# Two-layer transformer kernel: k, v and beta projected ahead of the first scan, q inside it; gates made at once; the last tile's loads and two layer-1 pieces placed later

## The chip, the cores and the metric

The kernel runs on one NeuronCore of a Trainium2 chip. The metric is the time of one execution on the device, in microseconds. Before the change it is 2255.97 us, the median of three runs (2253.57 to 2258.22).

The core has five engines, each with its own instruction queue, worked through in order: TensorE (PE, matrix products and transposes), VectorE (DVE), ScalarE (ACT, activation functions from tables that have to be loaded), GpSimd (POOL) and SyncE (SP). DMAs are issued here from the SP queue and from GpSimd's queue. All data is float32.

## The reference, cut to what matters

Eight sequences of 512 tokens with 256 features go through two layers. Layer 0 is a delta-rule attention, with a state of 16 x 16 per head that is updated token by token, followed by a mixture of eight experts with one expert per token. Layer 1 is a softmax attention with a position bias, followed by eight gated experts. Each branch is added to x with a gate made from a conditioning vector.

```python
mod = (silu(c) @ wmod).reshape(8, 6, 1, 256)          # for each layer
sa, ca, ga, sb, cb, gb = (mod[:, j] for j in range(6))
ga = (2 * (ga >= 0) - 1) * maximum(abs(ga), 0.25)     # gb alike
h = layernorm(x) * (1 + ca) + sa
q = l2norm(silu(h @ Wq.T)); k = l2norm(silu(h @ Wk.T))   # per head of 16
v = silu(h @ Wv.T); beta = sigmoid(h @ Wbeta.T)
def step(M, (q_t, k_t, v_t, b_t)):                    # over 512 tokens
    out_t = q_t @ M
    M = M + b_t * outer(k_t, v_t - M @ k_t)
x = x + ga * (rmsnorm(outs) @ Wo.T)
h = layernorm(x) * (1 + cb) + sb
x = x + gb * expert[argmax(h @ gate_w.T)](h)          # relu(h w1 + b1) w2 + b2
# layer 1: softmax attention, then gated experts, in the same frame
```

## The kernel before, in words

**Tiles and scans.** The tokens are cut into four tiles of 128 (index i), and a tile holds these 128 positions of all eight sequences (index b, called examples). For each tile `front(i, at)` makes q, k, v and beta, `heads` turns K and V so that the 128 pairs of example and head lie on the partitions, and `scan(i, K, V)` runs 128 steps. A step is four VectorE instructions, each of which needs the one before: product (L640), reduction (L644), product (L650), subtraction (L655). Every eighth step also copies eight columns of V into the buffer `terms` (L638), and every sixteenth one writes V back (L646). The outputs are not made step by step: `attend(i, ...)` makes them with matrix products during the next tile's scan, `route` then finds each token's expert and scatters the rows, and `experts` runs 15 slots of 128 rows. For each slot it loads the rows (L1061, SP queue) and the weights of the slot's expert (`fetch`, L1044, an indirect DMA on GpSimd's queue, two buffers for each of the two parts), multiplies (L1083, L1102), adds a bias on GpSimd (L1108) and stores (L1109, GpSimd's queue). The finished rows are gathered (L1117), multiplied by the gate (L1153) and added to x in memory (L1154), all on GpSimd's queue.

**Order.** The order is written by hand: each piece of work has a place, a step number, and `run` sorts the pieces and puts them between the scan's steps. The place binds VectorE's instructions of the piece to come after that step; the other engines' instructions are ordered by the framework's scheduler, by readiness and by the order of the code. So a piece whose other instructions are ready early can start early on them, while VectorE's instruction sits at its step and is waited for, or waits.

**front.** For the first tile (i = 0) everything runs ahead of the scan: `stats_first` (layer norm statistics of all eight examples), then for each example `turn` (normalise on ScalarE, L140; transpose, L143; scale and shift on ScalarE, L145), `project` (L535: 512 columns, q and k; L539: 272 columns, v and beta; silu, copy and squares on ScalarE) and `squares` (sums of squares by head on VectorE, L553). `roots` takes sigmoid and square roots on ScalarE and `scales` multiplies q, k and v by their factors per head (L588), for tile 0 on VectorE and GpSimd in turns, for the others on GpSimd. For tiles 1 to 3 the same pieces run inside the previous tile's scan, from step 30 (tile 1) or 47, with `stats` on ScalarE and `normal` (L517, L518) on VectorE.

**Gates.** `gate_rows` is called four times in the first scan (steps 6, 8, 14, 16): a matrix product gives 8 rows of 256, ScalarE copies them, four VectorE instructions make sign and magnitude (L367 to L370), and a DMA stores them for `load_gates` at step 26.

**The last tile.** `experts(3)` begins with the load of `x_last` (L1036), in a buffer of the tag `yrow`, of which there are two; the gathers of tile 2 use the same two buffers. In its middle it loads three tiles of x for layer 1 (L1113). `prologue` makes layer 1's first k, q and v from them: 14 pieces, of which the first eight (k = 0 to 7) are placed at 102 + 4k among the expert slots (placed at 10j), and the others at 201 + k. The pieces k = 6 and 7 are `both` (L261), q and k of the first three tiles.

Of the kernel before, what the change touches and what calls it, by code (L numbers as in the profile page):

```python
# [19 lines left out]
P = 128  # L20
B = 8
# [42 lines left out]
def tile_two_layers(ctx: ExitStack, tc: tile.TileContext, t: dict, out: bass.AP):  # L64
# [217 lines left out]
    with ExitStack() as l0:  # L282
# [68 lines left out]

        def gate_rows(layer, branch):

            wm = wms[layer, branch]
            pg = bank()
            for k in range(2):
                nc.tensor.matmul(
                    pg[:B, :D], scs[layer][:, k, :], wm[:, k, 2 * D :],
                    start=(k == 0), stop=(k == 1),
                )  # L360
            name = f"{layer}{branch}"
            g, sign, mag, gt = (
                fp.tile([B, D], F32, tag=tag, name=f"{tag}_{name}", bufs=2)
                for tag in ("hslot", "yrow", "ysb", "hTs")
            )
            nc.scalar.copy(g, pg[:B, :D])
            nc.vector.tensor_scalar(sign, g, 0.0, 2.0, ALU.is_ge, ALU.mult)  # L367
            nc.vector.scalar_tensor_tensor(mag, g, -1.0, g, ALU.mult, ALU.max)
            nc.vector.tensor_scalar_max(mag, mag, 0.25)
            nc.vector.scalar_tensor_tensor(gt, sign, -1.0, mag, ALU.add, ALU.mult)  # L370
            nc.gpsimd.dma_start(mod_d[f"g{name}"], gt)
# [77 lines left out]
        def front(i, at):  # L449
# [102 lines left out]
            def squares(b):  # L552
                nc.vector.tensor_reduce(  # L553
                    ss[:, :, b, :], got["sq", b].rearrange("p s (n d) -> p s n d", d=HD),
                    AX.X, ALU.add,
                )


            n = B if i == 0 else B // 2
# [8 lines left out]
            def scales(h):  # L568
                bs = slice(h * n, (h + 1) * n)
                nc.vector.tensor_scalar_add(ss[:, :, bs], ss[:, :, bs], 1e-6)  # L570
                nc.vector.reciprocal(ss[:, :, bs], ss[:, :, bs])
                nc.vector.tensor_mul(ss[:, 1, bs], ss[:, 1, bs], beta[:, bs])
                todo = [
                    (b, of)
                    for of in ((1, 2, 0) if i == 0 else ((1, 2, 0),))
                    for b in range(h * n, (h + 1) * n)
                ]
                for b, of in todo:
                    for which in of if i else (of,):
                        x, by = (  # L580
                            (qk[:, 0, b, :], ss[:, 0, b, :]),
                            (qk[:, 1, b, :], ss[:, 1, b, :]),
                            (v[:, b, :], beta[:, b, :]),
                        )[which]
                        view = x.rearrange("p (n d) -> p n d", d=HD)

                        ve = nc.vector if i == 0 and which and b % 2 else nc.gpsimd
                        ve.tensor_mul(view, view, by.unsqueeze(2).to_broadcast([P, NH, HD]))  # L588
# [18 lines left out]
            pieces = []  # L607
            for p in range(B // 2):
                if i > 0:
                    pieces.append((at + 8 * p, lambda p=p: stats(p)))  # L610
                    pieces.append((at + 8 * p + 4, lambda p=p: normal(p)))
                elif p == 0:
                    pieces.append((at, stats_first))
                for c in range(2):
                    b = 2 * p + c
                    pieces.append((at + 8 * p + 3 * c + 4, lambda b=b: turn(b)))

                    late = 4.5 if i == 0 else 0
                    pieces.append((at + 8 * p + 3 * c + 4 + late, lambda b=b: project(b)))
                    pieces.append((at + 8 * p + 3 * c + 11, lambda b=b: squares(b)))  # L620
            for h in range(B // n):
                last = at + 16 * h + (23 if i else 39)
                pieces.append((last, lambda h=h: roots(h)))
                pieces.append((last + 2, lambda h=h: scales(h)))
            pieces.append((at + 46, lambda: heads("K", qk[:, 1], 1.0)))
            pieces.append((at + 49, lambda: heads("V", v, -1.0)))
            got["qk"] = qk
            return got, pieces
# [28 lines left out]
        def attend(i, qk, V, x1, norms):  # L657
# [198 lines left out]
            for h in range(2):  # L856
                pieces.append((16 * h + 25, lambda h=h: roots(h)))
                for b in range(4 * h, 4 * h + 4):
                    pieces.append((13 * h + 25 + b, lambda b=b: rest(b)))
                    pieces.append((12 * h + 29 + b, lambda b=b: stats(b)))  # L860
# [170 lines left out]
        def experts(i, slot, idx):  # L1031


            if i == NT - 1:
                x_last = fp.tile([P, D], F32, tag="yrow", name="x_last", bufs=2)
                nc.sync.dma_start(x_last, x2d[0][i])  # L1036
# [37 lines left out]
            for j in range(NSLOT):  # L1074
# [36 lines left out]
                if i == NT - 1 and j == NSLOT // 2:  # L1111
                    for k in range(i):
                        nc.sync.dma_start(w1["xs"][:, k, :], x2d[0][k])  # L1113
# [128 lines left out]
        parts, pieces = front(0, 0)  # L1242
        run(pieces)
        rest, gathers = [], []
        for i in range(NT):
# [8 lines left out]
            else:  # L1254
# [9 lines left out]
                    (18, strip_rows),  # L1264
                    (26, load_gates),
                ]
            before = parts
            if i + 1 < NT:
                parts, more = front(i + 1, 47 if i > 0 else 30)
                pieces = pieces + more  # L1270
# [10 lines left out]
        for k, piece in enumerate(begun):  # L1281
            last.append((102 + 4 * k if k < NT + 4 else 201 + k, piece))
# [348 lines left out]
```

## Time and profile before

| | us |
|---|---|
| median of three runs | 2255.97 |
| the profiled execution, its own time | 2256.92 |
| its span, from first to last instruction | 2255.2 |
| before the first scan step (L655 at 66.5) | 66 |
| first to last scan step | about 1040 |
| from there to layer 1's first scores (1401.7) | about 295 |
| layer 1 | about 853 |

The mean granted TensorE clock is 0.864. A line of the timeline has the start in us from the span's start, the busy time in us, engine, line, operation, output and inputs by the program's names with shapes, the number of merged instructions, and in brackets the engine's idle time before it with what released it. "SPq" and "POOLq" are queue instructions. A line of the chain has start and length in us. A line of the waits has who waited for whom, the total in us, the number of times and the longest. A line of the busy times by stretch has the stretch, its length, busy us (and instructions) of PE, PE's weight loads, DVE, ACT and POOL, the granted clock, the DMA engines' busy share and GB/s.

### The profile page before, as it was taken

What the parts mean: (1) busy time and instruction counts of PE and PEld (TensorE: products, weight loads), DVE (VectorE), ACT (ScalarE), POOL (GpSimd) and SP (SyncE); (2) the same over time, 40 slices, a digit from 0 to 9 for tenths busy, and PEclk for the clock granted to TensorE, in tenths of its full rate; (3) what the DMA queues carried; (4) which work ended last, traced back from release to release, by engine and by line L of the source; (5) the groups of instructions that cost most, each with busy time, mean ns of one, the idle gap of its engine ahead of it and who ended that gap; (6) DMA issues with size and microseconds to landing.
All of it is one profiled execution on the core that took longest, in us unless ns stands there. A gap on an engine that the chain in (4) does not pass through costs nothing.

```text
span 2255.2 us, 32318 instructions
## 1 busy us (share of the span) xinstructions
PE 1726.5 (77%) x10874; PEld 1195.3 (53%) x10874; DVE 1595.2 (71%) x4533; ACT 1076.8 (48%) x2672; POOL 589.8 (26%) x791
## 2 busy tenths in 40 slices
PE   5334027479696887939893597999999999999997
PEld 3212025359574785738762596565555555555553
DVE  3899999899987999899652002686675767666654
ACT  5144025465356643613341244877475665747431
POOL 1102014145253453624374443010201011010111
PEclk9566567599798998959996798899999999999998
DMA  5110000178002680138665582000101010100001
GB/s 161 48 45 10 0 1 11 34 263 312 32 13 86 251 309 31 46 143 300 178 112 172 178 315 61 13 12 12 23 14 22 15 29 11 24 12 13 17 17 17
DMA packets 88630, 189.57 MB, mean 84 GB/s; under 512 B 13689, under 2 KB 67105, under 8 KB 75665
## 3 DMA queue, kind: packets, MB, share of 16 engines
q0 software_dynamic: 33696, 137.43, 19.0%
q1 hardware_dynamic: 54768, 50.09, 7.9%
q8 instruction: 86, 1.41, 0.3%
q14 instruction: 80, 0.65, 0.1%
HBM read 175.10 MB, written 36.93 MB: 94 GB/s over the span
## 4 chain that ended last, share of the span: by engine, by line
PE 42%; DVE 26%; issue 14%; ACT 7%; DMA 6%; POOL 5%; SPq 0%; POOLq 0%; ACTq 0%; DVEq 0%
PE ps L1469 6%; DVE state L644 6%; PE ps L1083 5%; PE ps L1330 5%; DVE state L655 5%; DVE terms L640 5%; DVE upd L650 5%; PE ps L1102 4%; PE ps L1304 3%; PE ps L535 3%; PE ps L1351 2%; DMA w<-in_wrows,idx 2%; PE ps L261 2%; DVE sc L1313 1%; PE ps L244 1%
## 5 line engine op out<-in xcount | busy, mean ns | idle before, releaser
L1318 ACT ACTIVATE pr<-sc,low 128x384 f32<-128x384 f32 (+3 forms) x512 | 255.6, 556 | 196.7 <-DVE low L1313 194.5
L1313 DVE CUSTOM_DVE_ANT_0 sc<-ps,strips 128x384 f32<-128x384 f32 (+3 forms) x512 | 225.4, 485 | 87.4 <-PE ps L1304 56.6
L1083 PE MATMUL ps<-hTs,w 128*128 128x128 f32 x1920 | 236.8, 284 | 19.9 <-DMA w<-in_wrows,idx 13.5
L1083 PEld LDWEIGHTS ps<-hTs,w 128*128 128x128 f32 x1920 | 233.3, 200 | 27.2 <-issue 13.1
L644 DVE TENSOR_REDUCE state<-terms 128x16 f32<-128x272 f32 x512 | 227.2, 444 | 15.8
L655 DVE TENSOR_TENSOR state<-state,upd 128x256 f32<-128x256 f32 x511 | 223.1, 437 | 14.8
L1469 PE MATMUL ps<-ew,hTd 128*128 128x512 f32 x512 | 232.9, 608 | 0.0
L640 DVE TENSOR_TENSOR terms<-state,K 128x256 f32<-128x256 f32 x512 | 216.0, 422 | 14.4
L1102 PE MATMUL ps<-w,act 128*128 128x256 f32 x960 | 220.8, 384 | 6.1 <-DVE dm L820 6.1
L650 DVE TENSOR_TENSOR upd<-K,state 128x256 f32<-128x256 f32 x511 | 214.2, 419 | 15.6
L1092 ACT ACTIVATE act<-ps,w 128x128 f32<-128x128 f32 x480 | 137.1, 371 | 152.8 <-PE ps L1083 151.7
L1330 PE MATMUL ps<-cst,pr 128*128 128x128 f32 x1280 | 192.4, 296 | 14.9 <-DVE low L1313 12.5
L1102 PEld LDWEIGHTS ps<-w,act 128*128 128x128 f32 x960 | 180.0, 193 | 29.5 <-DVE dm L820 6.6
L1474 DVE SCALAR_TENSOR_TENSOR accd<-ps,wtd,accd 128x256 f32<-128x256 f32 x256 | 123.8, 483 | 99.8 <-PE ps L1469 87.7
L1330 PEld LDWEIGHTS ps<-cst,pr 128*128 128x128 f32 x1280 | 149.8, 149 | 83.7 <-DVE low L1313 24.2
L1469 PEld LDWEIGHTS ps<-ew,hTd 128*128 128x128 f32 x512 | 96.4, 193 | 121.2 <-issue 107.6
L1478 POOL TENSOR_TENSOR accd<-accd,bc_g 128x256 f32<-128x256 f32 x28 | 20.4, 728 | 528.5 <-DVE accd L1474 528.5
L1044 POOL DMA_INDIRECT w<-in_wrows,idx x120 | 123.2, 1027 | 127.8 <-ACT hTs L1068 55.9
L1304 PE MATMUL ps<-kT,qTc 32*128 32x128 f32 (+3 forms) x1024 | 132.2, 491 | 5.4 <-DVE low L1313 3.8
L1339 DVE COPY prT<-ps 128x512 f32<-128x512 f32 (+3 forms) x256 | 117.0, 484 | 10.4 <-PE ps L1330 10.0
L674 PE MATMUL ps<-cst,V 128*128 128x128 f32 x64 | 12.5, 378 | 124.2 <-DVE V L646 124.2
L1337 ACT COPY prT<-ps 128x512 f32<-128x512 f32 (+3 forms) x256 | 98.9, 414 | 8.6 <-PE ps L1330 8.2
(264 smaller groups left out, 2939.4 us busy)
## 6 DMA issues: line engine op xcount, KB each, us to landing
hs<-zero SPq DMA_DIRECT2D x4, 1920.0 KB
hslot<-hs SPq DMA_DIRECT2D x60, 128.0 KB
ys<-ysb POOLq DMA_DIRECT2D x60, 128.0 KB, 3.8
x<-in_x SPq DMA_DIRECT2D x32, 128.0 KB
strips<-strip_d SPq DMA_DIRECT2D x16, 256.0 KB
out<-accd POOLq DMA_DIRECT2D x32, 128.0 KB, 3.1
wm<-in_wmod SPq DMA_DIRECT2D x4, 768.0 KB
xt<-in_x SPq DMA_DIRECT2D x12, 256.0 KB
```

Source lines behind the costliest of these rows:

```text
L640: nc.vector.tensor_mul(term[:, :, :HD], M, K[:, s, :].unsqueeze(1).to_broadcast([P, HD, HD]))
L644: nc.vector.tensor_reduce(delta, term, AX.X, ALU.add)
L650: nc.vector.tensor_mul(upd, K[:, s, :].unsqueeze(2).to_broadcast([P, HD, HD]), delta.unsqueeze(1).to_broadcast([P, HD, HD]),)
L655: yield nc.vector.tensor_sub(M, M, upd).ins
L1083: nc.tensor.matmul(ph[:, q * P : (q + 1) * P], w[:, k * FF + f * P : k * FF + (f + 1) * P], hT[:, k, :], start=(k == 0), stop=(k == 1),)
L1092: nc.scalar.activation(act[:, f, :], ph[:, q * P : (q + 1) * P], AF.Relu, bias=w[:, 2 * FF + f : 2 * FF + f + 1],)
L1102: nc.tensor.matmul(py[:, :D], act[:, f, :], w[:, f * D : (f + 1) * D], start=(f == 0), stop=(f == NFC - 1),)
L1304: made = nc.tensor.matmul(pscs[r][:, :W], qT[rows, g, o, i * P : (i + 1) * P], kT[rows, g, :W], start=True, stop=True,)
L1313: nc.vector.tensor_tensor_reduce(out=sc[:, :W], in0=pscs[r][:, :W], in1=strips[:, n, S - W :], scale=1.0, scalar=3.0e38, op0=ALU.add, op1= ...
L1318: nc.scalar.activation(pr, sc[:, :W], AF.Exp, bias=low, scale=-1.0)
L1330: nc.tensor.transpose(pt[:, (i - j) * P : (i - j + 1) * P], prs[r, i][:, j * P : (j + 1) * P], ident,)
L1469: nc.tensor.matmul(pe, hT[0][:, k, cols], ew[:, k, e : e + 2, :], start=(k == 0), stop=(k == 1),)
```

## The change

**First tile.** `front` gets pieces of its own for i = 0. `turn_first` normalises on VectorE and scales one half on ScalarE and the other on VectorE. `project_first` projects k, v and beta only; `squares_first` sums k's squares. q is projected, squared, summed and scaled by pieces in the list `later`, placed at steps 1 to 25 of the first scan, with sums and products on GpSimd. `scales_first` gives all v products to GpSimd and all k products to VectorE.

**Sums of squares.** `halved` sums 16 elements by four GpSimd adds on 8, 4, 2 and 1 columns per head. It is used for q of tile 0 and for tile 1; tiles 2 and 3 keep VectorE's reduction.

**Gates.** The four products are copied into one tile at partitions 0, 32, 64 and 96, and `push_gates` (step 20) makes all gates with four VectorE instructions and stores them with four DMAs.

**Places.** For tiles 1 to 3 `normal` comes one step later, `turn` one, `project`, `squares`, `roots`, `scales` and `heads` two; `attend`'s `stats` one. In the last tile `x_last` is loaded at slot 7 with layer 1's x, both behind the row loads issued so far; the pieces k = 6 and 7 of the prologue move to 151 and 152, behind the last slot.

```diff
+        gated = {}
         def gate_rows(layer, branch):
+            if not gated:
+                gated["g"] = fp.tile([P, D], F32, tag="hslot", name="gates", bufs=2)
+                nc.gpsimd.memset(gated["g"], 0.0)
...
-            nc.scalar.copy(g, pg[:B, :D])
+            at = 32 * (2 * layer + branch)
+            nc.scalar.copy(gated["g"][at : at + B, :], pg[:B, :D])
+        def push_gates():
...
             nc.vector.scalar_tensor_tensor(gt, sign, -1.0, mag, ALU.add, ALU.mult)
-            nc.gpsimd.dma_start(mod_d[f"g{name}"], gt)
+            for layer in range(2):
+                for branch in range(2):
+                    at = 32 * (2 * layer + branch)
+                    nc.gpsimd.dma_start(mod_d[f"g{layer}{branch}"], gt[at : at + B, :])
...
+            def turn_first(b):
...
+                nc.vector.tensor_scalar(
+                    xn, xt[:, q, :], rs[:, q : q + 1], off[:, q : q + 1], ALU.mult, ALU.add
+                )
...
+                nc.scalar.activation(
+                    hT[:, 0, :], pt[:, :P], AF.Identity, bias=plus[:, 0], scale=by[:, 0]
+                )
+                nc.vector.tensor_scalar(
+                    hT[:, 1, :], pt[:, P : 2 * P], by[:, 1], plus[:, 1], ALU.mult, ALU.add
+                )
+            def project_first(b):
...
+                for dst, lo, hi in ((pa, D, 2 * D), (pb, 2 * D, NQKV)):
...
+                nc.scalar.activation(qk[:, 1, b, :], pa[:, :D], AF.Silu)
+                nc.scalar.activation(v[:, b, :], pb[:, :D], AF.Silu)
+                nc.vector.tensor_copy(beta[:, b, :], pb[:, D : D + NH])
...
+            def scales_first():
...
+                for b in range(B):
+                    by_head(nc.gpsimd, v[:, b, :], beta[:, b, :])
+                    by_head(nc.vector, qk[:, 1, b, :], ss[:, 1, b, :])
...
+            def halved(dst, sq):
+                for m in (HD // 2, HD // 4, HD // 8):
+                    nc.gpsimd.tensor_add(sq[..., :m], sq[..., :m], sq[..., m : 2 * m])
+                nc.gpsimd.tensor_add(dst, sq[..., 0], sq[..., 1])
...
+            if i == 0:
+                pieces.append((0, stats_first))
+                for b in range(B):
+                    pieces.append((4 * b + 4, lambda b=b: turn_first(b)))
+                    pieces.append((4 * b + 9, lambda b=b: project_first(b)))
+                    pieces.append((4 * b + 13, lambda b=b: squares_first(b)))
+                    later.append((1 + 2 * b, lambda b=b: project_q(b)))
+                    later.append((4 + 2 * b, lambda b=b: squares_q(b)))
+                pieces += [(46, roots_first), (47, scales_first)]
+                later += [(22, roots_q), (25, scales_q)]
...
-                    pieces.append((12 * h + 29 + b, lambda b=b: stats(b)))
+                    pieces.append((12 * h + 30 + b, lambda b=b: stats(b)))
...
-            if i == NT - 1:
-                x_last = fp.tile([P, D], F32, tag="yrow", name="x_last", bufs=2)
-                nc.sync.dma_start(x_last, x2d[0][i])
...
                 if i == NT - 1 and j == NSLOT // 2:
-                    for k in range(i):
-                        nc.sync.dma_start(w1["xs"][:, k, :], x2d[0][k])
+                    x_last = fp.tile([P, D], F32, tag="yrow", name="x_last", bufs=2)
+                    with tc.issue_after(issued["rows"]):
+                        nc.sync.dma_start(x_last, x2d[0][i])
+                        for k in range(i):
+                            nc.sync.dma_start(w1["xs"][:, k, :], x2d[0][k])
...
-            last.append((102 + 4 * k if k < NT + 4 else 201 + k, piece))
+            place = 102 + 4 * k if k < NT + 2 else 145 + k if k < NT + 4 else 201 + k
+            last.append((place, piece))
```

## The prediction

> **What bounds the kernel now.** I read the chain of work that ended last first, then the busy times by stretch, then the timeline of the stretches that the change touches, and the waits there.
>
> ```profile
> PE 42%; DVE 26%; issue 14%; ACT 7%; DMA 6%; POOL 5%; SPq 0%; POOLq 0%; ACTq 0%; DVEq 0%
> 62.70:296.00 233.30, 57.87 (x189) 33.82 (x187) 217.40 (x534) 58.81 (x133) 16.90 (x29) 0.59 0.08 25
> ```
>
> No engine binds all of it. The last line is the first scan: VectorE busy 217.4 of 233.3 us, so a scan is a chain on VectorE, and everything put into its order is paid unless it fits the gaps between dependent instructions. The work before the first scan is bound by TensorE, then by a chain of ScalarE tables and products:
>
> ```profile
> 26.68 1.98 PE L535 MATMUL ps<-wqkv,hT 128*128 128x512 f32 x4 [0.69 <-ACT hT L145]
> 28.50 1.08 PE L539 MATMUL ps<-wqkv,hT 128*128 128x272 f32 x4
> ...
> 33.34 1.98 PE L535 MATMUL ps<-wqkv,hT 128*128 128x512 f32 x4 [0.69 <-ACT hT L145]
> ...
> 53.51 3.12 DVE L588 TENSOR_TENSOR qk<-qk,ss 128x256 f32<-128x256 f32 x4
> ...
> 57.91 3.68 PE L596 MATMUL ps<-cst,qk 128*128 128x128 f32 x16 [12.38 <-POOL qk L588]
> ```
>
> Two examples take 33.34 - 26.68 = 6.66 us; K's transposes wait 12.4 us, at the end for GpSimd, which scales q between its K products (L588, twelve products from 52.63, 8.12 us). The largest hole lies before the experts of the last tile (chain, then timeline, then the SP queue's waits):
>
> ```profile
> 1257.20 3.16 DMA x<-yrow
> 1260.49 0.34 SPq L1036
> 1260.87 3.10 DMA hslot<-hs
> ...
> 1264.10 0.66 PE L1064 MATMUL ps<-cst,hslot 128*128 128x128 f32 x2 [52.81 <-DMA hslot<-hs]
> ...
> SPq L1036 <- DMA x<-yrow: 42.2, 1, 42.2
> ```
>
> TensorE idles 52.8 us for a 128 KB load. That load is queued on SP behind x_last (L1036), and x_last waits 42.2 us, because its buffer (tag yrow, two of them) belongs to the third tile's gathers until their adds have landed. The scattered rows have been in place since about 1217, when the queue issues ew.
>
> **The change, part by part.** The sum is made against the profiled execution: span 2255.2, its own time 2256.9, so 1.7 us around the span. The median of the runs shown is 2256.0, 0.9 less; I take the savings from the profiled execution and give the forecast against the median.
>
> **Opening (turn_first, project_first, scales_first).** Today an example costs TensorE 1.82 us (L535, 26.68 to 28.50) and 0.91 us (L539), a transpose pair 0.30, and half of a 0.69 us wait per pair. Without q's 256 columns it is 0.91 + 0.91 + 0.30 = 2.12 us; turns run two examples ahead, so the wait goes. 3.33 - 2.12 = 1.21 us, seven times, is 8.5 us; the first example runs at the cold price (3.78 us for what costs 1.88 later), and I count nothing for it. ScalarE does four instructions of 0.37 to 0.47 us per example, 1.6 us; VectorE normalises (0.35, as the 128x256 tensor_scalar of L427), turns half (0.4), copies beta (0.17) and reduces half the squares (0.4), 1.3 us; both hide behind 2.12, and would cost the difference if that cover went. Tables and roots (46.3 to 49.6) stay. Then from the root to K's transposes it is 8.3 us. New: add, reciprocal and product at 128 columns, 0.2 + 0.94 + 0.6 = 1.8, and eight K products on VectorE. They cost 0.78 each beside GpSimd (53.51, 3.12 for four) and 0.42 alone; GpSimd's v products last 8 x 0.70 = 5.6 us, so 1.8 + 5.1 = 6.9 us, or 8.0 if something keeps GpSimd busy throughout. Gain 0.3 to 1.4, taken 1.0, since most products have company. **-9.5** (ends -6 and -11).
>
> **First scan.** Two rows of it (timeline of VectorE) and one of a later scan:
>
> ```profile
> 170.14 0.43 DVE L655 TENSOR_TENSOR state<-state,upd 128x256 f32<-128x256 f32 x1
> 170.49 0.67 DVE L553 TENSOR_REDUCE ss<-sq 128x32 f32<-128x512 f32 x1
> ...
> 518.42 3.68 DVE L638 COPY terms<-V 128x128 f32<-128x128 f32 x1
> ```
>
> A bare step is 1.86 us (66.48 to 68.34); this one, with a squares reduction, ends at 172.46 and is 2.32, so it costs 0.46, not 0.67. Eight go to GpSimd: -3.7. A step with four gate instructions is 2.53 (82.53 to 85.06), +0.67; four such groups become one of the same length per partition: -2.0. Added: q's add and reciprocal, +0.7 (the step with add, reciprocal and product is +1.06, of which the product is some 0.35). normal's waits for its root (1.2 us in this scan) are reached a step later: -0.6.
>
> GpSimd gets 40 instructions for q (32 adds, 8 products), 32 adds for tile 1, a memset; TensorE and ScalarE get q's 8 projections, roots. ScalarE is busy 58.8 us of 233 here, so this is hidden, if q's roots are there at step 25. VectorE waits for them there, and the whole scan is queued behind it. Eight projections at the cold price (1.9 us) and eight sums on GpSimd (no row; bounded by 0.61 us, the 128x256 product, for each of four adds, and 0.19, the small memset of L392, so 0.8 to 2.4 us an example, 1.1 taken since sizes halve) are done by about step 12. Tile 1's sums have some 4 us before their scales at step 57.
>
> Here a rule of the Trainium skill matters, and it speaks against the change. The row L638 is a copy of 0.27 us that took 3.68, all through GpSimd's run of products (517.9 to 522.5); at 790.40 another took 4.14. "SBUF — State Buffer", section "Who interferes with whom", has a port pair that VectorE's copies and GpSimd share, as a lock held for the whole instruction. By that a copy loses one GpSimd instruction at most, 0.6 us; by the rows it loses the rest of the run. The rows decide. About 27 us of new GpSimd work over 16 copies in 240 us is two hits: 0.6 us by the rule, up to 5 by the rows if they meet the 4.9 us run of q's products. That run begins at step 26, over by 29, and the copies stand at 24 and 32, so I take +1.2. Sum **-4.4** (ends -7 and 0).
>
> **Later scans: pieces one or two steps later.** The longest waits of the third scan:
>
> ```profile
> DVE stf L840 <- POOL x L832: 4.2, 4, 1.4
> DVE ss L553 <- ACT sq L549: 4.1, 3, 3.5
> ```
>
> The fourth scan has 4.3 on L840 again, the second 2.8 on L553 and 1.8 on L517. stats one step later saves up to 1.86 in each of two scans, the first squares up to 1.9 in two, normal 2.6 in all: -10 at most. What is late next is ScalarE's turn and project behind the later normal, so the squares gain less than their two steps. I take half, **-5**. The two long copies may lie better or worse against a run that starts two steps later: 0, ends -7 and +7.
>
> **Last tile's experts.** x_last moves from the head of experts to slot 7, behind that slot's row loads on SP. The loads follow ew, issued until 1218.2; with ew's 2 MB and three weight fetches in flight I let the first land at 1229, as the third fetch does (1229.7): 35 us earlier than 1264. What is queued behind the moved loads then is the later slots' rows; the gathers have landed by that time, so no wait. But GpSimd's queue is in order, and it is the one with the gathers: per slot a fetch 1.05, add 0.72, store 0.59, fetch 1.0 and four issue gaps of 0.3, so 4.6 of the slot's 7.24 us (1270.51 to 1277.75); the gathers need 8 x (1.0 + 0.74 + 0.95 + 0.9) = 29 us beside it. One end: all gathers go first, only the two slots whose weights are there by 1236.5 run early, and the third's fetch lands at 1268: -14.5 + 3 = -12. Other end: -35. Fetches are issued by readiness (one stands among the gathers at 1230.07), so some slots get through: I take three and a bit, **-22**. DMA has room, but not much: share 0.82 at 300 GB/s from 1265 to 1350.
>
> **q and k of layer 1's first three tiles (L261).** They stand between expert slots where TensorE has no gap:
>
> ```profile
> 1365.00 2.74 PE L261 MATMUL ps<-hTc,wqkv 128*128 128x384 f32 x8
> 1371.15 2.75 PE L261 MATMUL ps<-hTc,wqkv 128*128 128x384 f32 x8
> ```
>
> Moved behind the last slot they lie in the 10.1 us that TensorE waits for the gathered rows (to 1394.7). 2 x 2.58 = **-5.2**; without that cover 0. The gates' four stores at step 20 end at about 103 us; SP waits for them with the gates' load, and the next x tile behind it is not issued before 135.8 today, so 0.
>
> Sum: -9.5 - 4.4 - 5 - 22 - 5.2 = -46; 2256 - 46 = **2210**.
>
> **Rivals.** *GpSimd hands the early start back:* experts and gathers disturb each other, -8 to -12 in place of -22: 2222; for it the in-order queue, against it the fetch at 1230. *The scans' gains are eaten* by copies behind GpSimd runs and ScalarE's order: the 5 of the later scans and the 4.4 of the first gone, one or two long copies (3.5 each) more: 2222 to 2228. *Everything fits:* -34 at the experts, -8 in the scans: 2194. *The change doesn't do what it says* (another load holds SP): 2232. *Slower:* in tiles 1 to 3 the statistics of the next pair now stand between a pair's two projections. ScalarE's pair takes 16.2 us (134.64 to 150.84) against 15.8 of VectorE's steps. If that order forced two further table loads (2 x 1.28) and a second wait for the cold TensorE (2.2), each of 12 pairs would lose 4.8 us: 58, so 2268. It decides from (46 + 4.5) / 12 = 4.2 us a pair. Against: there are two loads a pair now (136.85, 148.61), and the new order also needs only two.
>
> **Chances.** Likeliest 0.55 (own range 2200 to 2220), handed back 0.15, eaten 0.10, everything fits 0.12, not as it says 0.03, slower 0.05. The range 2188 to 2234 holds all but the slow case and some tails. A change under 0.2% (4.5 us) can't be told from none here. Faster 0.94, same 0.01, slower 0.05.
>
> **What would show it.** First scan step at about 56 instead of 65.5; no L553 in the first scan; L1064 of the last tile near 1229 - 19 = 1210 with no SP wait on x<-yrow before it; L261 after the last L1102. It would be wrong if SP still waits there, if GpSimd's fetches come only after the gathers, or if copies of L638 show several microseconds in the first scan.

## The result, and the profile after

The changed kernel takes 2242.51 us (median of 17 runs, 2225.61 to 2246.34); the kernel before, run beside it, 2254.15 us (17 runs, 2248.09 to 2262.81). The ratio is 0.9933, with a 95% interval of 0.9916 to 0.9950: faster by 11 to 19 us. The forecast was 46 us faster, 2210, with a range of 2188 to 2234: the sign is right, the size is not.

The profiled execution took 2237.59 us with a span of 2235.7, so 19.5 less than the span before. The medians differ by 11.6: the profiled execution lies 4.9 us under the median of its runs, that of before 2.8 over its own, and in which part those 8 us lie is not shown. By parts, from the milestones of both traces (the first and last scan step, layer 1's first scores, the end):

| part | before, us | after, us | change | forecast |
|---|---|---|---|---|
| up to the first scan step | 66.5 | 55.6 | -10.9 | -9.5 |
| first scan | 249.7 | 244.9 | -4.8 | -4.4 |
| scans 2 to 4 | 789.7 | 795.4 | +5.7 | -5 |
| last scan's end to layer 1's first scores | 295.9 | 288.4 | -7.5 | -22 and -5.2 |
| layer 1 | 853.5 | 851.5 | -2.0 | 0 |

The first two rows are close to the forecast. This is the first scan in the busy times by stretch:

```profile
55.58:300.44 244.86, 59.37 (x195) 34.54 (x195) 227.15 (x556) 66.48 (x149) 44.80 (x101) 0.61 0.08 23
```

VectorE has 556 instructions here and GpSimd 44.8 us of work; in the whole first scan of before (66.48 to 316.16) it was 573 and 16.9 us. The opening, from the timeline:

```profile
29.64 1.95 PE L595 MATMUL ps<-wqkv,hT 128*128 128x256 f32 x8
31.42 0.38 PE L574 MATMUL ps<-cst,xn_first 128*128 128x128 f32 x2
...
40.73 6.04 POOL L619 TENSOR_TENSOR v<-v,beta 128x256 f32<-128x256 f32 x8 [38.07 <-ACT beta L614]
41.01 6.04 DVE L619 TENSOR_TENSOR qk<-qk,ss 128x256 f32<-128x256 f32 x8
47.20 1.52 PE L694 MATMUL ps<-cst,qk 128*128 128x128 f32 x6 [11.83 <-DVE qk L619]
```

An example costs TensorE 2.0 us (29.64 to 31.64) where 2.12 was forecast, and K's transposes begin at 47.20 in place of 57.91.

The third row went the wrong way. The waits of VectorE in the third scan, which before were led by 4.2 us (`stf`) and 4.1 us (the sums of squares):

```profile
DVE ss L680 <- ACT ss L676: 9.0, 1, 9.0
DVE count L1076 <- PE ps L1071: 3.5, 1, 3.5
DVE dm L925 <- POOL bdM L926: 2.1, 2, 1.4
DVE rsa L529 <- ACT sda L513: 2.0, 2, 1.7
DVE stf L945 <- POOL x L937: 0.9, 1, 0.9
```

The two waits that the change aimed at are down to 0.9 and nothing. At the head stands one that was 0.5 us before (L570 there, L680 now). The second scan has it too, with 10.1 us. Its surroundings, from the timeline:

```profile
450.90 0.69 PE L1166 MATMUL ps<-cst,hslot 128*128 128x128 f32 x2 [11.80 <-DMA hslot<-hs]
...
452.05 6.47 PE L1185 MATMUL ps<-hTs,w 128*128 128x128 f32 x32 [0.46 <-ACT hTs L1170]
...
458.36 0.38 PE L143 MATMUL ps<-cst,xna 128*128 128x128 f32 x2
...
460.11 1.98 PE L547 MATMUL ps<-wqkv,hT 128*128 128x512 f32 x4 [1.36 <-ACT hT L145]
...
465.60 0.31 ACT L676 ACTIVATE ss<-ss 128x128 f32<-128x128 f32 x1
...
465.94 0.23 DVE L680 TENSOR_SCALAR ss<-ss 128x128 f32<-128x128 f32 x1 [10.13 <-ACT ss L676]
```

Read it from the bottom: VectorE waits for a root of ScalarE; ScalarE, in order, has the silu and the squares of the next pair ahead of it; these wait for the pair's transposes and products (L143, L547); and TensorE, in order, first runs an expert slot (L1166, L1185), whose rows came after a wait of 11.8 us. Before, the order on TensorE was the other one:

```profile
463.28 0.69 PE L143 MATMUL ps<-cst,xna 128*128 128x128 f32 x2 [6.82 <-ACT xna L140]
464.52 3.78 PE L535 MATMUL ps<-wqkv,hT 128*128 128x512 f32 x4 [0.55 <-ACT hT L145]
468.09 1.59 PE L539 MATMUL ps<-wqkv,hT 128*128 128x272 f32 x4
469.52 0.38 PE L1064 MATMUL ps<-cst,hslot 128*128 128x128 f32 x2
```

Last, the last tile's experts, TensorE and GpSimd in the timeline:

```profile
1227.18 0.66 PE L1166 MATMUL ps<-cst,hslot 128*128 128x128 f32 x2 [21.83 <-DMA hslot<-hs]
...
1241.39 3.62 PE L1204 MATMUL ps<-w,act 128*128 128x256 f32 x16
...
1253.69 0.92 POOL L1259 DMA_DIRECT2D x<-yrow  x1 [0.30 <-POOL yrow L1258]
1254.91 1.10 POOL L1146 DMA_INDIRECT w<-in_wrows,idx  x1 [0.30 <-issue]
...
1261.00 1.41 PE L1185 MATMUL ps<-hTs,w 128*128 128x128 f32 x5 [15.99 <-DMA w<-in_wrows,idx]
```

The first slot starts 131.3 us after the last scan's end (158.2 before), so 26.9 sooner. Two slots run; then TensorE idles 16.0 us for weights whose fetch GpSimd issues at 1254.91, after its last gather's add. Counted from slot start to slot start, in us:

| slot | 0 | 1 | 2 | 3 to 5 | 6 | 7 to 10 | 11 | 12 | 13 | all 14 |
|---|---|---|---|---|---|---|---|---|---|---|
| before | 8.6 | 7.2 | 7.3 | 7.2 | 7.5 | 7.2 | 10.5 | 10.7 | 9.8 | 112.2 |
| after | 9.3 | 23.4 | 10.0 | 7.2 | 12.7 | 7.2 | 10.4 | 8.1 | 7.3 | 131.9 |

Slots 12 and 13 are shorter by 5.1 us: that is L261, which now lies behind the last slot, in the wait for the gathered rows:

```profile
1367.20 5.32 PE L261 MATMUL ps<-hTc,wqkv 128*128 128x384 f32 x16
1377.57 0.69 PE L179 MATMUL ps<-cst,xnc 128*128 128x128 f32 x2 [5.04 <-ACT xnc L172]
```

So of 26.9 us, 16.2 + 2.7 + 5.2 + 0.7 = 24.8 go back in slots 1, 2, 6 and 0. What delays slot 6 stands in ScalarE's rows (timeline):

```profile
1299.54 0.30 ACT L126 ACTIVATE sdc<-mvc,cst 128x3 f32<-128x3 f32 x1 [6.22 <-DVE mvc L121]
1299.75 1.12 ACT L1194 ACTIVATE act<-ps,w 128x128 f32<-128x128 f32 x4
...
1300.15 5.41 PE L1204 MATMUL ps<-w,act 128*128 128x256 f32 x16 [3.49 <-ACT act L1194]
```

The slot's ReLU (L1194) stands behind a root for layer 1 (L126), which waits for the x tiles that are now loaded only at slot 7. Before, these loads went out at 1261.9, ahead of the first slot.

### The profile page after: what moved, and what is told of

It reads as the page before. It is cut to its first block, busy times and chain, and to the rows that moved or that the text cites. A ratio compares the mean times of both kernels' runs of the same rounds, so it can differ in the third digit from the quotient of the medians.

```text
span 2235.7 us, 32456 instructions
## 1 busy us (share of the span) xinstructions
PE 1727.0 (77%) x10906; PEld 1205.2 (54%) x10906; DVE 1590.3 (71%) x4539; ACT 1090.1 (49%) x2678; POOL 615.1 (28%) x856
## 5 line engine op out<-in xcount | busy, mean ns | idle before, releaser
L1185 PE MATMUL ps<-hTs,w 128*128 128x128 f32 x1920 | 246.6, 291 | 35.2 <-DMA w<-in_wrows,idx 30.0
L1185 PEld LDWEIGHTS ps<-hTs,w 128*128 128x128 f32 x1920 | 242.7, 207 | 42.6 <-issue 32.5
L1194 ACT ACTIVATE act<-ps,w 128x128 f32<-128x128 f32 x480 | 136.8, 372 | 160.9 <-PE ps L1185 147.0
L1146 POOL DMA_INDIRECT w<-in_wrows,idx x120 | 123.6, 1030 | 132.9 <-ACT hTs L1170 64.2
L1446 DVE COPY prT<-ps 128x512 f32<-128x512 f32 (+3 forms) x256 | 117.1, 485 | 10.4 <-PE ps L1437 10.2
```

Of the source, the lines that this page charges most:

```text
L1185: nc.tensor.matmul(ph[:, q * P : (q + 1) * P], w[:, k * FF + f * P : k * FF + (f + 1) * P], hT[:, k, :], start=(k == 0), stop=(k == 1),)
L1194: nc.scalar.activation(act[:, f, :], ph[:, q * P : (q + 1) * P], AF.Relu, bias=w[:, 2 * FF + f : 2 * FF + f + 1],)
```

## The experiments

All kernels start from the changed one. The time up to layer 1's first scores is given first (1401.7 before, 1384.3 after), since the code of layer 1 is the same in all and its time varies from 842 to 855 us (last section); then the median and the ratio to the kernel before on the same chip.

### Where scans 2 to 4 lost

In the changed kernel the third pair of examples has `turn` at 47 + 16 + 5 = 68, and the first expert slot is placed at 68 too; the slot's piece is earlier in the list, so it goes first. Before, `turn` and `project` were at 67. The first kernel moves the slots of tiles 0 and 1:

```diff
-                        pieces.append((68 + pace * (j + half / 2), on))
+                        pieces.append((68 + 1.5 * (i < NT - 2) + pace * (j + half / 2), on))
```

> The changed kernel, with the expert slots of tiles 0 and 1 placed 1.5 steps later (69.5 in place of 68), so that the turn and projection of the third pair (steps 68 and 69 since the change, 67 before it) stand ahead of the first slot again in TensorE's queue. Theory 1 (the places of the change put the third pair behind the slot on TensorE, so ScalarE's root of the sums comes late and VectorE waits at step 75): the waits of 10.1 and 9.0 us before L680 in scans 2 and 3 go, scans 2 and 3 take 262 to 266 us each in place of 272.6 and 273.6, and the whole is 12 to 18 us under the changed kernel: some 2227 where that has 2242. Theory 2 (ScalarE is simply late because everything was placed two steps later): the waits stay at 8 us or more, the whole within 4 us of the changed kernel.

First scores at 1366.2; 2221.72 us (2218.86 to 2229.01), ratio 0.9869 (0.9847 to 0.9891). Scans 2 to 4 take 261.2, 268.4 and 249.3, together 778.9: 16.5 less than the changed kernel and 10.8 less than the kernel before. From the timeline of the second scan:

```profile
448.86 3.78 PE L547 MATMUL ps<-wqkv,hT 128*128 128x512 f32 x4 [0.55 <-ACT hT L145]
...
453.59 0.38 PE L1166 MATMUL ps<-cst,hslot 128*128 128x128 f32 x2
...
456.33 0.31 ACT L676 ACTIVATE ss<-ss 128x128 f32<-128x128 f32 x1
...
456.68 0.23 DVE L680 TENSOR_SCALAR ss<-ss 128x128 f32<-128x128 f32 x1 [1.23 <-ACT ss L676]
```

The pair is ahead of the slot, and the wait of 10.13 us is 1.23 (9.0 is 1.0 in the third scan). Theory 1 holds; the third scan stayed 2 us over what it expected. By the two ratios the whole is 14 us shorter.

The second puts the places of tiles 1 to 3 back as before; the third does that and moves the slots as well.

```diff
-                        pieces.append((at + 8 * p + 5, lambda p=p: normal(p)))
-                    pieces.append((at + 8 * p + 3 * c + 5, lambda b=b: turn(b)))
-                    pieces.append((at + 8 * p + 3 * c + 6, lambda b=b: project(b)))
-                    pieces.append((at + 8 * p + 3 * c + 13, lambda b=b: squares(b)))
+                        pieces.append((at + 8 * p + 4, lambda p=p: normal(p)))
+                    pieces.append((at + 8 * p + 3 * c + 4, lambda b=b: turn(b)))
+                    pieces.append((at + 8 * p + 3 * c + 4, lambda b=b: project(b)))
+                    pieces.append((at + 8 * p + 3 * c + 11, lambda b=b: squares(b)))
...
-                    last = at + 16 * h + 25
+                    last = at + 16 * h + 23
...
-                    pieces.append((12 * h + 30 + b, lambda b=b: stats(b)))
+                    pieces.append((12 * h + 29 + b, lambda b=b: stats(b)))
```

`heads` of tiles 1 to 3 go back to +46 and +49.

> The changed kernel, with all places of tiles 1 to 3 as before the change (normal, turn, project, squares, roots, scales, heads of those tiles, and the statistics of attend). Theory 1 (the later places cost more than they bring): scans 2 to 4 together return from +5.6 us to about 0 against the kernel before, the waits before L680 go and the waits on L840's like (4 us) and on the squares come back; the whole 4 to 8 us under the changed kernel, some 2237. The forecast's step (later places are worth 5 us): scans 2 to 4 as before the change, and the whole 5 us over the changed kernel. Halved sums for tile 1 on GpSimd remain, so their own effect is left in the first scan's end and in scan 2.

First scores at 1376.5; 2229.57 us (2223.64 to 2235.80), ratio 0.9903 (0.9881 to 0.9926). Scans 2 to 4: 265.5, 273.6, 252.3, together 791.4, close to before (789.7) and 4.0 less than in the changed kernel, as theory 1 has it; the rest of the 7.8 us gained at the first scores lies behind the last scan, where the code is the same. The old waits are back, and with them the two long copies:

```profile
502.89 3.69 DVE L743 COPY terms<-V 128x128 f32<-128x128 f32 x1
```

and 4.16 us at 775.81, as 3.68 and 4.14 before the change. With the later places and later slots the same two copies take 1.47 and 1.49 us, but two others take 1.73 each (0.33 here), so that all 48 copies of these scans take 19.5 us there and 22.0 here. In the changed kernel's first scan none of the sixteen is longer than usual (mean 0.271 us).

> The changed kernel with the places of tiles 1 to 3 put back as before the change, and the slots of tiles 0 and 1 at 69.5. Theory 1 (the later places themselves bring the gain once the third pair is ahead of the slot): scans 2 to 4 together stay at 789 to 793 us as with the places put back alone (791.4), against 778.9 with the later places and later slots. Theory 2 (the later slots bring it): 778 to 783.

First scores at 1378.6; 2220.25 us (2217.32 to 2225.01), ratio 0.9851 (0.9828 to 0.9874). Scans 2 to 4: 788.7, so the later slots alone bring 2.7 of the 12.5 us between 791.4 and 778.9, and the later places 9.8. Theory 1, a little under its band. The gain is in the waits: VectorE is idle for 78.2 us of these scans here and 69.5 with the later places. Its waits for GpSimd's x ahead of the statistics (L945) fall from 8.5 to 1.8 us and those for the squares (L666) from 7.8 to nothing; others grow, and the copies take 3 us more.

The 9.8 us are shown for the scans, not for the whole: the ratios, 0.9851 here and 0.9869 with the later places, do not differ beyond their intervals. Layer 1 took 844.6 us here and 854.8 there, and the mean granted clock is 0.875 or 0.876 in all four runs here, 0.866 to 0.870 in all six there. Why is open.

### Where the earlier start went

The loads put back: `x_last` at the head of `experts(3)`, layer 1's x at slot 7 without waiting for rows.

```diff
+            if i == NT - 1:
+                x_last = fp.tile([P, D], F32, tag="yrow", name="x_last", bufs=2)
+                nc.sync.dma_start(x_last, x2d[0][i])
...
-                    with tc.issue_after(issued["rows"]):
-                        nc.sync.dma_start(x_last, x2d[0][i])
-                        for k in range(i):
-                            nc.sync.dma_start(w1["xs"][:, k, :], x2d[0][k])
+                    for k in range(i):
+                        nc.sync.dma_start(w1["xs"][:, k, :], x2d[0][k])
```

> The changed kernel, with x_last loaded at the head of the last tile's experts as before, and layer 1's three x tiles at slot 7 without waiting for the rows. Theory 1 (the earlier start is handed back: 16.0 us of TensorE wait before slot 2, 2.8 before slot 3, 5.4 before slot 7): the first slot starts some 27 us later again, those three waits go, and the whole is only 1 to 5 us over the changed kernel. Forecast's step: 22 us over it.

First scores at 1389.3, 5 us later; 2240.99 us (2238.90 to 2243.16), ratio 0.9954 (0.9937 to 0.9971). The first slot starts 27.6 us later after the last scan, and slots 1, 2 and 6 take 7.2, 7.3 and 7.2 again. So the early start is worth 4 to 5 us as it is in the changed kernel, not 22.

The third tile's gathers between the last tile's slots:

```diff
-                gathers += behind
+                gathers += behind if i < NT - 1 else []
...
         run(rest + gathers + strips + more)
+        last += [(2 + 8 * n, piece) for n, (_, piece) in enumerate(behind)]
...
-                    with tc.issue_after(issued["scatter" if i == NT - 2 else "fetch"]):
+                    with tc.issue_after(issued["fetch"]):
```

> The changed kernel, with the third tile's nine gather steps placed among the last tile's slots (2 + 8n in the order where slot j stands at 10j), each issued behind the last weight fetch before it, so that the fetches of slots 2 and 3 come ahead of most gathers on GpSimd's queue. Theory 1 (the wait of 16.0 us before slot 2 is GpSimd's queue working through the gathers first): the wait falls below 6 us; GpSimd then has 4.6 us for a slot and some 3.6 for a gather, over TensorE's 7.24, so slots 2 to 7 take up to 8.5 each; net 6 to 14 us under the changed kernel. Rival (the DMA engines are full then, the weights come late whatever the order): slots 0 to 7 together take the same time within 3 us, the wait only spread.

First scores at 1373.8; 2222.94 us (2217.91 to 2228.74), ratio 0.9877 (0.9856 to 0.9898). Slots 0 to 3 take 9.6, 7.3, 7.2 and 7.3: the waits of 16.0 and 2.8 us are gone. Slots 4 to 8 take 9.2, 12.1, 9.8, 9.6 and 8.6, more than the 8.5 expected. The 14 slots take 121.4 in place of 131.9. In GpSimd's rows the fetch for slot 2 goes out at 1235.67, where it was 1254.91, with only one gather ahead of it and the second behind:

```profile
1235.67 1.07 POOL L1146 DMA_INDIRECT w<-in_wrows,idx  x1 [10.05 <-ACT hTs L1170]
...
1241.69 0.98 POOL L1222 DMA_INDIRECT yrow<-ys,slot  x1 [0.30 <-PE ps L1166]
```

That GpSimd's queue held the fetch is shown; a part of the time comes back in slots 4 to 8.

Layer 1's pieces kept behind the slot at which they stand on ScalarE, alone:

```diff
-                        nc.scalar.activation(
+                        issued["relu"] = nc.scalar.activation(
                             act[:, f, :], ph[:, q * P : (q + 1) * P], AF.Relu,
                             bias=w[:, 2 * FF + f : 2 * FF + f + 1],
-                        )
+                        ).ins
...
-            last.append((place, piece))
+            def bound(piece=piece):
+                with tc.issue_after(issued["relu"]):
+                    piece()
+            last.append((place, bound))
```

> The changed kernel with layer 1's prologue pieces bound behind the ReLU of the slot at which they stand. Theory 1 (the slot before slot 7 takes 12.7 us in place of 7.2 because ScalarE, in order, waits there for layer 1's x tiles, which are loaded 36 us later than before relative to the first slot): it takes 7.2 to 7.6, and layer 1's first scores come 5 us earlier, at 1379. Rival (the weights of slot 7 are late, behind these loads): it stays over 10 us.

First scores at 1382.1; 2231.14 us (2228.56 to 2236.23), ratio 0.9906 (0.9879 to 0.9932). Slot 6 takes 7.2 us in place of 12.7, so ScalarE's order was the cause. The 14 slots take 127.6, 4.3 less; the first slot starts 2.2 us later after the scan than in the changed kernel's profile, where nothing differs, so only 2.1 show at the first scores.

The edits of the slots, the gathers and this one together:

> The changed kernel with three edits: the slots of tiles 0 and 1 at 69.5; the third tile's gathers between the last tile's slots (2 + 8n); and layer 1's prologue pieces bound behind the ReLU of the slot at which they stand, so that ScalarE does not reach the root of layer 1's statistics (L126 now) before slot 10. Theory 1 (three separate queue effects that add up): layer 1's first scores come 16 us earlier for the slots, 10 for the gathers and 2 to 5 for the wait of 5.4 us before slot 7, so near 1354 in place of 1384.3, and the whole is 28 to 32 us under the changed kernel, some 2208 where that has 2239. Rival (they cover each other, because after the first edit the rows and fetches meet more traffic): less than 22 us.

First scores at 1358.0; 2213.95 us (2211.24 to 2219.95), ratio 0.9840 (0.9818 to 0.9862). At the first scores 26.3 us are gained, between the two expectations (21 by the two ratios, which is in the rival's band): 19.4 in scans 2 to 4 and 7.8 behind them, less 0.9 ahead of them. Slots 4 to 8 still take 8.9, 13.1, 10.2, 9.2 and 10.4.

Then `ew`, 2 MB for layer 1, out of SP's way, and the gathers at 11 + 7.5n:

```diff
-        for k in range(2):
-            nc.sync.dma_start(
-                ew[:, k], t["expert_w"][:, k * P : (k + 1) * P, :].rearrange("e p d -> p e d")
-            )
...
+        def load_ew():
+            for k in range(2):
+                with tc.issue_after(issued["rows"]):
+                    nc.sync.dma_start(
+                        w1["ew"][:, k],
+                        t["expert_w"][:, k * P : (k + 1) * P, :].rearrange("e p d -> p e d"),
+                    )
+        last.append((142, load_ew))
         run(last)
```

> As the kernel with three edits, and the 2 MB load of layer 1's expert weights (ew), which stands on SP ahead of the last tile's rows, is issued behind the rows of the last slot; the gathers at 11 + 7.5n. Theory 1 (the first slot's rows wait for ew's packets: issued at 1211.4, landed at 1227): the first slot starts 8 to 15 us sooner after the last scan's end than the 132.5 us of the changed kernel, and the whole is another 6 to 14 us shorter, some 2198. Rival (the first slots' own weights, three fetches of 1.1 MB, are as late): the first slot starts sooner, but slots 0 to 3 wait for weights, net under 3 us. If the late load of ew meets layer 1's beginning, its first use comes long after (no loss).

First scores at 1346.1; 2201.93 us (2188.77 to 2205.69), ratio 0.9769 (0.9741 to 0.9796). The first slot starts 117.8 us after the last scan's end (131.3 in the changed kernel), 11.9 sooner than with the three edits, and all of that arrives. The SP queue's rows of the changed kernel show the order that is gone:

```profile
1210.94 0.40 SPq L212 DMA_DIRECT2D ew<-in_expert_w  x2
1211.39 16.80 SPq L1163 DMA_DIRECT2D hslot<-hs  x3
```

The first rows were issued 0.4 us behind `ew` and came late because of it. That the gathers moved too does not explain it: moving them by themselves, in the kernel with the gathers between the slots, left the first slot at 131.4. Slots 4 to 9 stay long: 9.1, 12.0, 9.6, 9.2, 11.9, 10.2.

Last, VectorE takes GpSimd's products of the gathered rows and the slots' bias adds:

```diff
-                nc.gpsimd.tensor_add(ysb, ysb, w[:, NFC * D :])
+                (nc.vector if i == NT - 1 else nc.gpsimd).tensor_add(ysb, ysb, w[:, NFC * D :])
...
-                    nc.gpsimd.tensor_mul(yr, yr, gates[1][:, k, :])
+                    made = (nc.vector if i == NT - 2 else nc.gpsimd).tensor_mul(yr, yr, gates[1][:, k, :])
+                    issued["mul"] = made.ins
```

> As the kernel with ew late, and VectorE takes the gate products of the third tile's gathered rows and the bias adds of the last tile's slots from GpSimd; layer 1's prologue pieces are also bound behind the last of these products. Theory 1 (GpSimd's queue paces slots 4 to 9 there: 4.6 us for a slot and 3.6 for a gather, over 7.24): with 3.6 and 2.6 left it fits, slots 4 to 9 go from 9.1, 12.0, 9.6, 9.2, 11.9 and 10.2 us to at most 8.2 each, and layer 1's first scores come 10 to 16 us earlier than 1346. Rival (the DMA engines are the limit: 2.2 MB of weights, 0.4 MB of rows in a slot): less than 4 us.

First scores at 1342.8; 2197.25 us (2182.80 to 2202.18), ratio 0.9742 (0.9713 to 0.9771). Slots 4 to 9 take 7.5, 12.8, 9.0, 9.8, 9.2 and 7.9: 5.8 us less together, where 13 or more were expected, and 3.3 at the first scores. The busy times of this stretch (slots 3 to 9), and under them those of the same slots in the kernel before:

```profile
1221.20:1285.40 64.20, 54.34 (x351) 49.11 (x349) 6.62 (x19) 20.74 (x71) 31.51 (x34) 0.97 0.92 314
1288.30:1339.20 50.90, 50.90 (x352) 47.84 (x351) 0.00 (x0) 20.45 (x70) 23.45 (x28) 1.00 0.92 343
```

By its number the rival holds (less than 4 us), but its cause is not shown. In the kernel before the DMA engines are as busy, 0.92, and TensorE never waits: weights and rows alone fit in 7.2 us a slot. What comes on top here is the traffic of the gathers and of layer 1's x tiles: by the two lines 20.2 MB in 64.2 us, where it was 17.5 MB in 50.9. At the 343 GB/s of before, 20.2 MB would take 59 us (an estimate), so the added bytes would account for some 8 of the 13.3 us. GpSimd's queue is not free of waits either: at 1237.33 and 1243.57 a gather has waited 2.5 and 2.1 us for an add to x to land, each with a weight fetch behind it. What each of these costs is open. This version is 2.3 to 2.9% under the kernel before, and faster than the changed one.

### q and k of layer 1 back between the slots

```diff
-            place = 102 + 4 * k if k < NT + 2 else 145 + k if k < NT + 4 else 201 + k
+            place = 102 + 4 * k if k < NT + 4 else 201 + k
```

> The changed kernel with the two pieces of layer 1's q and k (L261) back between the last tile's slots, at 126 and 130. Forecast's step (2.6 us each, in a place where TensorE has no gap): slots 12 and 13 take 10 to 10.7 us again in place of 8.1 and 7.3, and layer 1's first scores come 5.2 us later, at 1389.5. Rival (they fill waits anyway): under 1 us.

First scores at 1393.0; 2244.62 us (2232.36 to 2255.80), ratio 0.9968 (0.9952 to 0.9984). Slots 12 and 13 take 10.7 and 9.8 us in place of 8.1 and 7.3: 5.1, as forecast. The other 3.7 at the first scores come before these slots, where the kernels are the same.

### Sums of squares, and the first tile alone

```diff
-                if i == 1:
-                    halved(ss[:, :, b, :], sq)
-                else:
-                    nc.vector.tensor_reduce(ss[:, :, b, :], sq, AX.X, ALU.add)
+                nc.vector.tensor_reduce(ss[:, :, b, :], sq, AX.X, ALU.add)
```

and the same for q in `squares_q`.

> The changed kernel with the sums of squares of tile 0's q and of tile 1 back on VectorE as reductions. Theory 1 (a reduction in the first scan costs its own length there, 0.46 us for 512 columns and some 0.3 for 256): the first scan is 5 to 6 us longer than 244.9, and the whole likewise. Rival (GpSimd's forty adds cost VectorE as much in waits): less than 2 us longer.

First scores at 1391.5; 2241.70 us (2233.87 to 2250.33), ratio 0.9945 (0.9925 to 0.9966). The first scan takes 251.7 us in place of 244.9: +6.9, over the band. The groups of VectorE in that scan show why:

```profile
L664 DVE TENSOR_REDUCE ss<-sq 128x32 f32<-128x512 f32 x8 | 5.4, 674 | 0.0
L650 DVE TENSOR_REDUCE ss<-sq_q 128x16 f32<-128x256 f32 x8 | 3.3, 409 | 1.0 <-ACT sq_q L639 1.0
```

The reductions take 8.7 us by themselves. They overlap their neighbours, so VectorE is busy 6.0 us longer (233.2 for 227.2) and idle 0.9 longer. The whole does not settle it: by the two ratios it is 2.7 us longer, and the intervals overlap. In the changed kernel no wait of VectorE in this scan is for GpSimd's adds.

The last one puts the places, the loads and the L261 pieces back together, and leaves the opening, q in the first scan, the gates and the sums:

> The changed kernel with the places of tiles 1 to 3, the loads of the last tile and the two q and k pieces put back as before the change: what is left are the opening, the first scan with q, the gates made at once and the sums on GpSimd. Forecast's steps (opening -9.5, first scan -4.4): first scan step near 56, first scan 245 us, scans 2 to 4 within 3 us of the 789.7 before, last tile within 3 us of before; layer 1's first scores at 1386 to 1389 in place of 1401.7, and the whole 12 to 16 us under the kernel before. Rival (gains of the opening are given back later, since scans and slots wait for the same loads): under 8 us.

First scores at 1393.5; 2249.58 us (2231.49 to 2254.63), ratio 0.9967 (0.9945 to 0.9990). First scan step at 57.1, first scan 244.3, scans 2 to 4 791.0: at the last scan's end 13.5 us are gained, as forecast. Between there and layer 1's first scores 5.3 are lost (301.1 for 295.9), though the code there is the one before. The median gain is 7.4 us (2.3 to 12.4): under the expected 12 to 16 and in the rival's band, though the interval just reaches 12. The scatter of the rows begins 102.6 us after the last scan's end, 99.5 before; in the kernels run here this varies from 97.1 to 103.2 with no order that the edits explain. Whether that is chance or a cost of the earlier tile is open, so the rival's reason is not shown.

## Why the prediction was wrong, and where it was right

**Right:** the opening (-9.5 forecast, -10.9 measured; the first step at 55.6 and no sums of squares in VectorE's first scan, as it had said), the first scan (-4.4 and -4.8), and L261 (-5.2 and -5.1, with the cover that it named). In the first scan's sum two small terms were off and partly cancel, so that its closeness is in part luck: the long copies, +1.2, did not come, and `normal`'s waits for its root, -0.6, did not shrink (1.2 us before, 1.5 after). That a copy loses the rest of GpSimd's run of products and not one of its instructions, the reading of the rows that the prediction preferred to the rule of the Trainium skill ("SBUF — State Buffer", section "Who interferes with whom"), agrees with the copies of 3.69 and 4.16 us that come back when the places are put back: the first, from 502.89, ends at 506.58, as the last of the products that GpSimd runs from 501.19 to 507.01 has begun.

**Wrong, later scans (-5 forecast, +5.7 measured).** The failed sentence is "What is late next is ScalarE's turn and project behind the later normal". It followed the pair through its own pieces and did not ask which other piece has the same number. One step later meant 68, the step of the first expert slot, and in TensorE's queue the pair fell behind a slot that waits for its rows. Two waits of 10.1 and 9.0 us took the place of the gain. With the order restored the later places bring 9.8 us in these scans, nearly the -10 that the forecast had as its end: the mechanism was right and sized too low, and a tie turned it into a loss.

**Wrong, the last tile (-22 forecast, -2.3 measured without L261).** Three terms failed. *The start:* 35 us earlier was assumed, 26.9 came. The loads were let land "with ew's 2 MB and three weight fetches in flight" at 1229 in the old count, 123 us after the last scan; it was 131, and with `ew` out of the way it is 118: the term had `ew` in flight and gave it no delay of this size. *The fetches:* "Fetches are issued by readiness, so some slots get through: I take three and a bit". None got through: the one fetch among the gathers, in both profiles, is for slot 1, and that of slot 2 stood behind all eight gathers. With the gathers between the slots the wait went, as the experiment shows. The end that the prediction gave for this case, -12, was the right picture; the later start and slot 6 took most of it. *Not seen:* the three x tiles that move along with `x_last`. The prediction counted who waits on SP for them and not who waits on ScalarE: 5.2 us in slot 6.

Three readings in the working were off as well. The stretch 62.70:296.00 is not the whole first scan (VectorE busy 232.7 of 249.7 us). The first step before the change is at 66.5, not 65.5. And "DMA has room", a share of 0.82, is a mean over a longer stretch; over slots 3 to 9 it is 0.92, so there was less room for gathers among the slots than that share says.

**The rivals.** "GpSimd hands the early start back" and "the scans' gains are eaten" both happened in part. The first came for its stated reason and was larger than stated (19.7 us for 10 to 14). Of the second only the later scans' gain went, for an order on TensorE; the first scan kept its own. Each was worked out with the rest of the forecast intact, 2222 and 2222 to 2228. The two losses as measured make 2210 + 19.7 + 10.7 = 2240, which is near the measured time and outside the range. The slow rival's 58 us did not come, but its further table loads did, against "the new order also needs only two": ScalarE loads a table 14 times in each of scans 2 and 3, where it was 10 (12 with the slots later, 10 with the places back), 1.28 us each. Two of them, at 460.42 and 464.30, stand in the chain behind the wait of 10.1 us. With the slots later, most of their cost is hidden: those scans are shorter than before all the same.

## What to carry to other kernels

When a piece moves by a step, look for every other piece with that step number, on every engine that the piece uses: a tie at one place can put short work behind a long wait. When a load is moved up, follow the next thing its consumer needs through the in-order queue that issues it, and list also what was moved with it. Mechanisms that are listed as rivals can come true together, and the range has to hold their sum.

## What was not expected of the hardware

**Much of the spread goes with the granted TensorE clock.** Over the 17 runs of the changed kernel the time falls as the mean granted clock rises, from 2246 at 0.866 to 2226 at 0.878 (correlation -0.87). Over 62 runs of the kernel before, the correlation is -0.72, with 9 us per 0.01. In the profiles the difference lies in layer 1, which is the same in all: 855 us at a clock of 0.96 there, 842 at 0.98. Differences between two medians of less than some 5 us are therefore read here from the parts of the profile. These vary too: where the code is the same, by some 1 us up to the last scan's end, and by 6 us from there to the scatter of the rows. The spread need not be chance alone: of the two kernels with the slots of tiles 0 and 1 later, with and without the later places, all runs of one have a lower clock than all runs of the other.

**A row load of 128 KB behind 2 MB.** Of two loads issued 0.4 us apart on the same queue the small one was read by TensorE 15.8 us after its issue (1211.39 to 1227.18). With the large one gone it was 5.0 us (1189.70 to 1194.67). Whether the delay arises in the queue or in the DMA engines is not separated here.
